# Gated delta-rule block on one core: convolution taps read an SBUF copy of the projection instead of PSUM

## The chip, the cores and the metric

The kernel runs on one core of a Trainium2 chip. A core has five engines which work side by side, each on its own in-order queue: TensorE (PE in the profile; its weight loads are PEld) multiplies matrices and writes to PSUM, VectorE (DVE), ScalarE (ACT) and GpSimd (POOL) work elementwise, and SyncE (SP) issues most of the transfers. The metric is the device time of the whole program in microseconds; less is better. Everything is 32-bit floating point.

## The reference

The input is 16 sequences of 128 tokens with 256 features. Three parts follow each other: an attention, a gated delta rule (where the change lies) and a feed-forward part with low-rank adapters and weights rounded to 8 bits. Cut to what matters here:

```python
x = x + delta_rule(attention(x, ...), W_qkv, W_z, W_b, W_a, conv_w, ...)
x = x + quantized_ffn(lora_ffn(x, ...), ...)

def delta_rule(hidden_states, ...):
    mixed = hidden_states @ W_qkv
    mixed = silu(causal_conv(mixed, conv_w))       # four taps over time, each channel by itself
    q, k, v = split(mixed)                         # 16 key heads, 32 value heads, 128 wide
    core = chunk_gated_delta_rule(q, k, v, g, beta)
    core = core * rsqrt(mean(core * core)) * norm_w * silu(z)
    return core.reshape(b, s, VAL_DIM) @ W_out

def causal_conv(x, w):
    out = xp[:, 0:s, :] * w[:, 0]                  # xp: x with three zeros in front of the time axis
    for j in range(1, 4):
        out = out + xp[:, j:j + s, :] * w[:, j]

def chunk_gated_delta_rule(q, k, v, g, beta):
    q, k = l2norm(q), l2norm(k)                    # x * rsqrt(sum(x * x) + eps)
    A = tril(-(k_beta @ k.T) * decay, -1)
    T = solve_triangular(eye - A, eye)             # the inverse of each 64-token chunk's matrix
    ...
```

## The kernel before

The delta rule is cut into 64 units, one for each of 16 key heads and each of 4 groups of 4 sequences; a unit has 8 pairs of a sequence and a value head (two value heads share a key head). A unit's work is a chain of steps over some ten slots. The loop at lines 853 to 910 makes the slots: in slot n the keys of unit n are made (`keys`, lines 471 to 510), the decays of unit n-1 are applied (`decays`, lines 512 to 545), unit n-7 gets its inverse merged and its values (`mergers`, `values`), unit n-8 its outputs, unit n-10 its last projection (`finish_unit`). In every fourth slot, and the one after, the 32x32 inverses of four units are worked out by VectorE and GpSimd (`inverse`, lines 547 to 642). For the first slots the rest of the attention is mixed in, and after the last slot comes the feed-forward part from line 915 on.

`plan` (lines 859 to 860) gives each step of a slot a due time between 0 and 24; the steps are called in the order of these times. A due time is thus a rank and not a clock. The program's framework then lists the instructions of each engine: it takes the steps' order as priority, but an instruction whose inputs it expects to be ready earlier may come ahead of one of higher priority. On the chip each engine works through its list in order and waits where an input or a buffer is missing.

The steps that the prediction speaks of:

- `conv` (lines 459 to 469) makes a projection of 128 channels by 512 tokens on TensorE into one PSUM buffer (`mm_in`, line 455), multiplies it by the last tap on ScalarE (line 464, the tile `cv`), and adds the other three taps on VectorE (line 466), each of which reads the PSUM buffer again, shifted by 1 to 3 tokens. It runs four times a slot: qk(0) and qk(1) in `keys`, val(0) and val(1) in `values` (line 715).
- `silu` (line 483) writes keys and queries to `kq`; `square` (line 487) squares all of `kq` with one instruction into a tile `sqa` of its own; `norms` (lines 489 to 495) sums the squares over the channels with products against a matrix of ones, four blocks of 32 partitions, and VectorE turns the result.
- `products` (lines 526 to 535) multiplies keys with keys and queries, and VectorE multiplies the result by the decays into `bT` and `aT`. `diagonal` sends the 32x32 diagonal blocks by four DMAs to the tile `diag`, from which `inverse` begins.
- `fades` (lines 436 to 450) prepares the decays of two units at once in every even slot: GpSimd lines 443 and 444, twice, and an exponential on ScalarE (line 448).
- `norm` in `outputs` (lines 772 to 777) scales the gated output on GpSimd; `turn` and `project` in `finish_unit` transpose it and multiply it by the output weights.
- PSUM tiles with the tag `b` share six buffers; a slot asks for 23 of them in turn. A buffer is given out again when its last reader is through. `cv` has three buffers in SBUF.
- `ffn_loads` (lines 816 to 827), called in slot 66, loads the first weights of the feed-forward part into tiles that are free by then, the first adapter among them (into `sqa`'s place) and the first group's residual (into `diag`'s place). The residuals of the other groups are loaded from line 926 on.

Of the kernel before, what the change touches and what calls it, by code (L numbers as in the profile page):

```python
# [8 lines left out]
F32 = mybir.dt.float32  # L9
I32 = mybir.dt.int32  # L10
AF = mybir.ActivationFunctionType
# [45 lines left out]
def tile_adaln_attn_ffn(  # L57
# [401 lines left out]
    def conv(g, w, blk, col):  # L459

        ps = mm_in(g, w, blk)
        cv = pc.tile([P, GS, S], F32, name="cv", tag="cv", bufs=3)
        psv = ps.rearrange("p (s t) -> p s t", t=S)
        A.activation(cv, psv, AF.Copy, scale=cw[:, col, 3:4])  # L464
        for sh in (1, 2, 3):
            V.scalar_tensor_tensor(out=cv[:, :, sh:], in0=psv[:, :, : S - sh],  # L466
                                   scalar=cw[:, col, 3 - sh : 4 - sh], in1=cv[:, :, sh:],
                                   op0=ALU.mult, op1=ALU.add)
        return cv

    def keys(u):
# [4 lines left out]
        def qk(j):  # L476

            if j == 0:
                d["kq"] = pa.tile([P, GS, 2, S], F32, name="kq", tag="kq", bufs=2)
            d["kc", j] = conv(g, w_qk[u], 1 - j, NK + kh if j == 0 else kh)  # L480

# [3 lines left out]
        def square():  # L485
            d["sqa"] = pa.tile([P, GS, 2, S], F32, name="sqa", tag="sqa")
            A.activation(d["sqa"], d["kq"], AF.Square)

        def norms():

            ps = ps_b.tile([P, 2 * GS, BL], F32, name="ps_n", tag="b")
            for b in BLOCKS:
                T.matmul(ps[b], lhsT=ones, rhs=d["sqa"][:, :, :, b], start=True, stop=True)
            d["tr"] = pc.tile([P, 2 * GS, BL], F32, name="turned", tag="turned")
            V.transpose(out=d["tr"].rearrange("p s t -> p (s t)"), in_=ps.rearrange("p s t -> p (s t)"))  # L495

        def factors():
            tr = d["tr"][:, :, 0].rearrange("p (s j) -> p j s", j=2)
            nn = d["nn"] = pc.tile([P, 2, GS], F32, name="nn", tag="nn", bufs=10)
# [207 lines left out]
    def values(u):  # L707
# [4 lines left out]
        def val(h):  # L712
            if h == 0:
                d["v"] = late["p"].tile([P, GS, 2, S], F32, name="v", tag="v", bufs=2)
            d["vT", h] = conv(g, w_v[u], h, 2 * NK + 2 * kh + h)

# [99 lines left out]
    def ffn_loads():  # L816
        def loaded(name, src, tag, **kw):
# [7 lines left out]
        adapter(0, pa.tile([P, GS * LA + LB], F32, name="adapters", tag="prod"),  # L825
                pa.tile([P, GS * LA], F32, name="firsts", tag="sqa"))()
        residual(0, pa.tile([P, GS, D], F32, name="x1_in", tag="diag"))

# [10 lines left out]
    def residual(g, t):  # L839
        nc.sync.dma_start(out=t, in_=x1[g * GS : (g + 1) * GS].rearrange("b s d -> s b d"))  # L840
        pre["x", g] = t
# [11 lines left out]
    for n in range(N + LAST):  # L853
# [31 lines left out]
        if at(MERGE) or at(MERGE + 1):  # L885
            steps = mergers(at(MERGE), at(MERGE + 1))
            plan(steps, [0, 0, 8, 14] if at(MERGE) else [14])
        if at(1):
            plan(decays(at(1)), [0, 4.5, 9, 10])
        if at(0):  # L890
            plan(keys(at(0)), [2, 5, 6.0, 10, 12.0, 14, 19])
        if n % 2 == 0 and n < N:
            plan(fades(n), [8, 12, 19])
        if at(MERGE):
            plan(values(at(MERGE)), [5.5, 8.5, 9, 15.5, 18, 23])
        if at(OUT):
            plan(outputs(at(OUT)), [13, 20, 16, 17, 19, 22, 23.5])
        if at(LAST):
            plan(finish_unit(at(LAST)), [0, 8, 14, 14])
        if at(NU + 1) and (n - NU - 1) % NU == 0:  # L900
# [14 lines left out]
    with ExitStack() as st:  # L915
# [9 lines left out]

        for g in range(1, NG):
            residual(g, w3.tile([P, GS, D], F32, name=f"x1_in{g}", tag=f"x1_in{g}"))
# [220 lines left out]
```

## Time and profile before

| | us |
|---|---|
| median of three runs | 2430.25 |
| lowest and highest run | 2428.03, 2436.76 |
| profiled execution: device time | 2431.28 |
| its span, first to last instruction | 2429.6 |
| busy: TensorE, VectorE, ScalarE, GpSimd | 2200.7, 1548.1, 1361.7, 1145.9 |
| conv: taps on VectorE, line 466 (768 instructions) | 540.2 |
| conv: scales on ScalarE, line 464 (256) | 174.5 |
| squares on ScalarE, line 487 (64) | 67.2 |

Busy time of one engine is a sum over the whole program. An instruction row names line, engine and operation, then the tile written, an arrow and the tiles read, then the sizes as partitions x elements. What stands in brackets behind a row of a timeline is the idle time of the engine before it and what ended it; a row of waits has the waiting instruction, what it waited for, and total us, times and longest wait. Matmul ends in the profile are modelled, so times between starts say more than single durations.

### The profile page before, as it was taken

What the parts mean: (1) busy time and instruction counts of PE and PEld (TensorE: products, weight loads), DVE (VectorE), ACT (ScalarE), POOL (GpSimd) and SP (SyncE); (2) the same over time, 40 slices, a digit from 0 to 9 for tenths busy, and PEclk for the clock granted to TensorE, in tenths of its full rate; (3) what the DMA queues carried; (4) which work ended last, traced back from release to release, by engine and by line L of the source; (5) the groups of instructions that cost most, each with busy time, mean ns of one, the idle gap of its engine ahead of it and who ended that gap; (6) DMA issues with size and microseconds to landing.
All of it is one profiled execution on the core that took longest, in us unless ns stands there. A gap on an engine that the chain in (4) does not pass through costs nothing. (4 is left out here: it accounts for less than half of the span.)

```text
span 2429.6 us, 41939 instructions
## 1 busy us (share of the span) xinstructions
PE 2200.7 (91%) x16248; PEld 1450.2 (60%) x16248; DVE 1548.1 (64%) x2102; ACT 1361.7 (56%) x3008; POOL 1145.9 (47%) x833
## 2 busy tenths in 40 slices
PE   7868759989999998989999998989999898999999
PEld 3433336766667666766666666766677686344445
DVE  4657878687776968687777868687876831311111
ACT  3566536766666666766666666766666574111110
POOL 4585535465555656465555656465556413700000
PEclk9889879999999999999999999999999999999999
DMA  1200022222222322322223222222322323000000
GB/s 56 91 17 15 24 56 76 70 66 71 68 66 77 104 72 64 75 68 68 68 80 86 82 73 64 77 66 68 85 69 80 89 52 123 26 0 20 9 0 18
DMA packets 289910, 148.37 MB, mean 61 GB/s; under 512 B 184241, under 2 KB 278193, under 8 KB 289713
## 3 DMA queue, kind: packets, MB, share of 16 engines
q1 hardware_dynamic: 287792, 141.44, 21.1%
q0 software_dynamic: 1344, 4.20, 0.5%
q8 instruction: 131, 2.15, 0.4%
q14 instruction: 67, 0.54, 0.1%
q10 hardware_dynamic: 576, 0.05, 0.0%
HBM read 119.13 MB, written 5.51 MB: 51 GB/s over the span
## 5 line engine op out<-in xcount | busy, mean ns | idle before, releaser
L466 DVE SCALAR_TENSOR_TENSOR cv<-ps_in,cw,cv 128x500 f32<-128x500 f32 (+2 forms) x768 | 540.2, 735 | 88.8 <-ACT cv L464 84.2
L455 PE MATMUL ps_in<-hT,w_v 128*128 128x512 f32 x512 | 281.5, 679 | 6.8 <-DVE z L770 4.6
L464 ACT ACTIVATE cv<-ps_in,cw 128x512 f32<-128x512 f32 x256 | 174.5, 682 | 182.7 <-PE ps_in L455 182.0
L770 DVE TENSOR_TENSOR z<-ps_ot,z 128x512 f32<-128x512 f32 x128 | 87.9, 687 | 289.9 <-ACT sq L768 289.9
L455 PE MATMUL ps_in<-hT,w_qk 128*128 128x512 f32 x512 | 251.3, 613 | 7.1 <-DVE z L770 6.2
L743 PE MATMUL ps_z<-w_gate,hT 128*128 128x256 f32 x1024 | 242.3, 379 | 1.7 <-DVE z L770 1.7
L800 PE MATMUL ps_out<-wo_head,zT 128*128 128x256 f32 x1024 | 238.8, 386 | 1.0 <-ACT zT L792 1.0
L500 POOL TENSOR_SCALAR nn<-turned 128x4 f32<-128x4 f32 x64 | 15.6, 244 | 419.4 <-DVE turned L495 316.8
L800 PEld LDWEIGHTS ps_out<-wo_head,zT 128*128 128x128 f32 x1024 | 189.0, 190 | 38.0 <-issue 10.7
L743 PEld LDWEIGHTS ps_z<-w_gate,hT 128*128 128x128 f32 x1024 | 189.4, 190 | 27.7 <-DVE z L770 2.6
L455 PEld LDWEIGHTS ps_in<-hT,w_v 128*128 128x128 f32 x512 | 104.6, 217 | 113.3 <-issue 105.2
L768 ACT ACTIVATE sq<-ps_ot 128x128 f32<-128x128 f32 x512 | 143.2, 280 | 31.6 <-PE ps_ot L762 23.0
L483 ACT ACTIVATE kq<-cv 128x512 f32<-128x512 f32 x128 | 80.1, 626 | 126.8 <-DVE cv L466 126.7
L756 ACT COPY y<-ps_y 128x512 f32<-128x512 f32 x128 | 75.0, 586 | 135.3 <-PE ps_y L755 130.6
L530 PEld LDWEIGHTS ps_kq<-kq 128*128 128x128 f32 x512 | 102.5, 203 | 73.4 <-issue 53.4
L455 PEld LDWEIGHTS ps_in<-hT,w_qk 128*128 128x128 f32 x512 | 94.2, 195 | 84.8 <-issue 67.0
L1055 POOL TENSOR_TENSOR o<-o,x_in 128x512 f32<-128x512 f32 x8 | 10.1, 1265 | 283.4 <-DVE o L1054 283.4
L777 POOL TENSOR_TENSOR z<-z,r 128x1024 f32<-128x1024 f32 x64 | 132.2, 2066 | 23.2 <-DVE z L770 20.4
L790 PE MATMUL ps_zt<-ident,z 128*128 128x128 f32 x512 | 88.9, 301 | 59.4 <-DVE aT L534 57.4
L530 PE MATMUL ps_kq<-kq 128*128 128x256 f32 x512 | 136.8, 391 | 0.0
L762 PE MATMUL ps_ot<-y,aT 128*128 128x128 f32 x1024 | 135.3, 275 | 0.0
L755 PEld LDWEIGHTS ps_y<-v,W 128*128 128x128 f32 x1024 | 123.3, 194 | 16.6 <-ACT W L701 10.8
(212 smaller groups left out, 5004.2 us busy)
## 6 DMA issues: line engine op xcount, KB each, us to landing
aT<-sums SPq DMA_DIRECT2D x64, 512.0 KB, 5.8
w_qk<-in_w_qkv_dram SPq DMA_DIRECT2D x128, 128.0 KB, 2.2
w_v<-in_w_qkv_dram SPq DMA_DIRECT2D x64, 256.0 KB, 2.7
w_gate<-in_w_z_dram SPq DMA_DIRECT2D x64, 256.0 KB, 2.7
wo_head<-in_w_out_dram SPq DMA_DIRECT2D x64, 256.0 KB, 2.7
diag<-bT SPq DMA_DIRECT2D x256, 32.0 KB, 2.0
W<-Uc SPq DMA_DIRECT2D x256, 32.0 KB, 2.0
T<-Tc SPq DMA_DIRECT2D x128, 32.0 KB, 1.9
```

The lines of the kernel that those rows point to most:

```text
L455: T.matmul(ps, lhsT=w[:, c, blk, :], rhs=hTs[g][:, c, :], start=c == 0, stop=c == ND - 1)
L464: A.activation(cv, psv, AF.Copy, scale=cw[:, col, 3:4])
L466: V.scalar_tensor_tensor(out=cv[:, :, sh:], in0=psv[:, :, : S - sh], scalar=cw[:, col, 3 - sh : 4 - sh], in1=cv[:, :, sh:], op0=ALU.mult, ...
L530: T.matmul(ps[:, j, :, :], lhsT=d["kq"][:, s, 0, :], rhs=d["kq"][:, s, :, :], start=True, stop=True)
L743: T.matmul(ps[:, j, :], lhsT=hTs[g][:, c, t0 : t0 + S], rhs=w_gate[u][:, c, :], start=c == 0, stop=c == ND - 1)
L755: T.matmul(ps[:, j, :], lhsT=d["W"][:, p, :], rhs=v[:, p, :], start=True, stop=True)
L762: T.matmul(ps[:, j, :], lhsT=d["aT"][:, p, :], rhs=d["y"][:, p, :], start=True, stop=True)
L768: A.activation(sq, ps[:, j, :], AF.Square, accum_out=d["r"][:, p : p + 1])
L770: V.tensor_tensor(z, ps, z, ALU.mult)
L777: G.tensor_tensor(d["z"], d["z"], d["r"][:, :, None].to_broadcast([P, NP, S]), ALU.mult)
L790: T.transpose(ps[:, j, :], d["z"][:, 4 * n + j, :], ident)
L800: T.matmul(ps[:, j, :], lhsT=d["zT", n][:, 2 * j + h, :], rhs=w_o[u][:, h, :], start=kh == j == h == 0, stop=kh == NK - 1 and j == h == 1)
```

## The change

`conv` first copies the PSUM buffer to an SBUF tile `raw` on ScalarE (four buffers). All four taps read `raw`: ScalarE's scale, and VectorE's three, whose two tensor inputs, `raw` and `cv`, are now both in SBUF. `cv` has two buffers instead of three. `conv` returns `raw` too; for keys and queries the squares are written into it, by one instruction for each, so that `sqa` goes. `norms` takes the two tiles apart, with eight products of half the width in place of four, and `factors` reads the sums in that order. The first adapter's raw rows take `diag`'s place in `ffn_loads`, and the first group's residual is loaded with the others after the slots. Most due times are changed.

```diff
     def conv(g, w, blk, col):
         ps = mm_in(g, w, blk)
-        cv = pc.tile([P, GS, S], F32, name="cv", tag="cv", bufs=3)
-        psv = ps.rearrange("p (s t) -> p s t", t=S)
-        A.activation(cv, psv, AF.Copy, scale=cw[:, col, 3:4])
+        raw = pc.tile([P, GS, S], F32, name="raw", tag="raw", bufs=4)
+        A.copy(raw, ps.rearrange("p (s t) -> p s t", t=S))
+        cv = pc.tile([P, GS, S], F32, name="cv", tag="cv", bufs=2)
+        A.activation(cv, raw, AF.Copy, scale=cw[:, col, 3:4])
         for sh in (1, 2, 3):
-            V.scalar_tensor_tensor(out=cv[:, :, sh:], in0=psv[:, :, : S - sh],
+            V.scalar_tensor_tensor(out=cv[:, :, sh:], in0=raw[:, :, : S - sh],
                                    scalar=cw[:, col, 3 - sh : 4 - sh], in1=cv[:, :, sh:],
                                    op0=ALU.mult, op1=ALU.add)
-        return cv
+        return cv, raw
...
-            d["kc", j] = conv(g, w_qk[u], 1 - j, NK + kh if j == 0 else kh)
+            d["kc", j], d["sqa", j] = conv(g, w_qk[u], 1 - j, NK + kh if j == 0 else kh)
...
         def square():
-            d["sqa"] = pa.tile([P, GS, 2, S], F32, name="sqa", tag="sqa")
-            A.activation(d["sqa"], d["kq"], AF.Square)
+            for j in range(2):
+                A.activation(d["sqa", j], d["kq"][:, :, j, :], AF.Square)
         def norms():
             ps = ps_b.tile([P, 2 * GS, BL], F32, name="ps_n", tag="b")
-            for b in BLOCKS:
-                T.matmul(ps[b], lhsT=ones, rhs=d["sqa"][:, :, :, b], start=True, stop=True)
+            for j in range(2):
+                for b in BLOCKS:
+                    T.matmul(ps[b, GS * j : GS * (j + 1), :], lhsT=ones, rhs=d["sqa", j][:, :, b], start=True, stop=True)
...
-            tr = d["tr"][:, :, 0].rearrange("p (s j) -> p j s", j=2)
+            tr = d["tr"][:, :, 0].rearrange("p (j s) -> p j s", j=2)
...
-            d["vT", h] = conv(g, w_v[u], h, 2 * NK + 2 * kh + h)
+            d["vT", h], _ = conv(g, w_v[u], h, 2 * NK + 2 * kh + h)
...
-                pa.tile([P, GS * LA], F32, name="firsts", tag="sqa"))()
-        residual(0, pa.tile([P, GS, D], F32, name="x1_in", tag="diag"))
+                pa.tile([P, GS * LA], F32, name="firsts", tag="diag"))()
...
-            plan(steps, [0, 0, 8, 14] if at(MERGE) else [14])
+            plan(steps, [1, 5, 8, 15] if at(MERGE) else [15])
         if at(1):
-            plan(decays(at(1)), [0, 4.5, 9, 10])
+            plan(decays(at(1)), [0, 2.5, 8, 13])
         if at(0):
-            plan(keys(at(0)), [2, 5, 6.0, 10, 12.0, 14, 19])
+            plan(keys(at(0)), [2, 4.5, 5.5, 10, 12.0, 14, 19])
         if n % 2 == 0 and n < N:
-            plan(fades(n), [8, 12, 19])
+            plan(fades(n), [10, 13.0, 21])
         if at(MERGE):
             plan(values(at(MERGE)), [5.5, 8.5, 9, 15.5, 18, 23])
         if at(OUT):
-            plan(outputs(at(OUT)), [13, 20, 16, 17, 19, 22, 23.5])
+            plan(outputs(at(OUT)), [15, 22, 17.5, 20, 21, 23, 24])
         if at(LAST):
-            plan(finish_unit(at(LAST)), [0, 8, 14, 14])
+            plan(finish_unit(at(LAST)), [0, 6, 11, 12])
...
-        for g in range(1, NG):
+        for g in range(NG):
             residual(g, w3.tile([P, GS, D], F32, name=f"x1_in{g}", tag=f"x1_in{g}"))
```

The lists of due times name the steps in the order in which their functions return them: `mergers` place, lower, grow, last; `decays` weight, products(0), products(1), diagonal; `keys` qk(0), qk(1), silu(0), silu(1), square, norms, factors; `fades` log(0), log(1), exp; `values` val(0), val(1), silu(0), silu(1), val_turn(0), val_turn(1); `outputs` gate(0), gate(1), new_values(0), new_values(1), attend(0), attend(1), norm; `finish_unit` turn(0), turn(1), project(0), project(1).

## The prediction

> **What bounds the kernel now.** The page comes first, for the shares; then the busy time by stretch, the waits of the tensor engine, and the timelines of four neighbouring slots.
>
> ```profile
> span 2429.6 us, 41939 instructions
> PE 2200.7 (91%) x16248; PEld 1450.2 (60%) x16248; DVE 1548.1 (64%) x2102; ACT 1361.7 (56%) x3008; POOL 1145.9 (47%) x833
> ```
>
> TensorE is nearly full, but 91% is a mean. A slot is the time from one unit's first `w_qk` product to the next one's. From about 490 us to 1858 us the slots repeat in groups of four, 12.6 groups in all; one group, busy time by stretch:
>
> ```profile
> core 0: us, PE busy (x) PEld busy (x) DVE busy (x) ACT busy (x) POOL busy (x), PEclk, DMA share, GB/s
> 984.50:1008.70 24.20, 24.20 (x226) 18.05 (x225) 12.63 (x20) 16.14 (x42) 7.93 (x8) 1.00 0.24 61
> 1008.70:1034.80 26.10, 24.69 (x227) 17.95 (x225) 21.19 (x37) 21.39 (x49) 15.84 (x13) 1.00 0.35 92
> 1034.80:1063.60 28.80, 25.98 (x224) 18.91 (x224) 28.63 (x31) 16.02 (x41) 16.41 (x10) 0.94 0.20 50
> 1063.60:1093.60 30.00, 26.76 (x225) 18.93 (x226) 19.46 (x24) 20.36 (x44) 19.67 (x15) 0.94 0.30 82
> ```
>
> Call the rows A, B, C, D. In A TensorE never pauses: 24.2 us is the price of a slot by TensorE alone. Four of them are 96.8 us; the group takes 109.1. So 12.3 us a group, 155 us in all, is the most that this stage can give. C has VectorE busy for 28.63 of 28.80 us: the inverse of the 32x32 blocks runs there. The waits of TensorE name the same place:
>
> ```profile
> PE ps_zt L790 <- DVE aT L534: 57.4, 26, 2.6
> ...
> PE ps_n L493 <- ACT sqa L487: 24.3, 22, 5.6
> PE ps_up L681 <- DVE z L770: 20.1, 13, 2.5
> ```
>
> These are PSUM buffers (six under tag `b`) which VectorE returns late. In C, VectorE's timeline and then TensorE's:
>
> ```profile
> 1040.52 1.06 DVE L578 TENSOR_TENSOR prod<-inv,gm 128x512 f32<-128x512 f32 x1
> 1041.51 0.73 DVE L466 SCALAR_TENSOR_TENSOR cv<-ps_in,cw,cv 128x508 f32<-128x508 f32 x1
> ...
> 1043.42 0.67 DVE L534 TENSOR_TENSOR aT<-ps_kq,aT 128x512 f32<-128x512 f32 x1
> ```
> ```profile
> 1044.24 1.09 PE L790 MATMUL ps_zt<-ident,z 128*128 128x128 f32 x4 [2.56 <-DVE aT L534]
> ```
>
> ScalarE had the first tap ready at 1037.47; VectorE took it up at 1041.51, 4.0 us late, and TensorE stood 2.56 us. Its next products are slow as well (the `ps_in` row after it takes 2.96 us for a usual 1.88, the clock of the stretch is 0.94): some 1.5 us more. D loses 0.3, 1.28 and 1.90 us the same way and 1.9 to the clock, B 0.71 (squares late) and 0.70.
>
> **What the Trainium skill says.** "SBUF — State Buffer", Who interferes with whom: a VectorE instruction with two SBUF inputs contends with a GpSimd instruction that reads SBUF, and the one that starts second waits until the other is through; with one SBUF input it does not. The trace agrees. The 128x128 scalar_tensor_tensor of line 330 reads two SBUF tiles:
>
> ```profile
> L330 DVE SCALAR_TENSOR_TENSOR a<-a,ea x4: 273/916/2014, 98.3 to 328.7; 128x128 f32<-128x128 f32 x4
> ```
> ```profile
> 183.05 1.90 POOL L256 TENSOR_TENSOR sc<-sc,mx 128x1024 f32<-128x1024 f32 x1 [3.90 <-PE ps_qk L202]
> ```
>
> Its slowest instance starts at 183.08 and takes 2.01 us instead of 0.27, ending just after GpSimd's. Today's taps read PSUM and one SBUF tile, and their means by form are 729 to 740 ns with no such tail. "TensorE: Matmul & The Clock Gate", What's actually happening: an idle window drops TensorE to half its clock; the slow products after the 2.56 us stall agree.
>
> **The change part by part.** The profiled execution is 2431.28 us, 1.7 outside its span; the sum starts there. The median of the runs is 2430.25.
>
> *Copies, scales, squares (ScalarE).* 256 copies of 128x512 from PSUM at 586 ns (the row of line 756) are +150 us. The 256 scales now read SBUF: today 682; the SBUF row of line 718 has 626 without a per-partition scale; I take no change, -14 to +14 us. 128 squares at about 630 (strided, as line 483) for 64 at 1050: +13. ScalarE goes from 1361.7 to some 1525 us, 63%: not a bound, but 2.6 us a slot in an in-order queue.
>
> *The taps (VectorE).* 768 instructions stay. Shorter from SBUF? Line 290 (PSUM, per-partition scalar) takes 344 at 128 elements, line 330 (SBUF, immediate) 273. At most -70 ns, 54 us of VectorE work; at worst 0. No row parts the memory from the scalar, so I take 0.
>
> *PSUM comes back earlier: gain.* Four of a slot's 23 buffers are returned by a 0.59 us copy. In C, TensorE then waits for `aT` at grow instead of turn(1): from the end of products(0) the run ahead is 1.72 + 0.63 + 1.72 + 0.49 = 4.6 us (rows of `ps_in`, `ps_lo`, `ps_in`, `ps_zt`) against 4.2 today; and bT, aT no longer stand behind two taps (1.3 us). Some 1.6 us more lateness is borne in C and in D[...]: -1.6 - 1.5 in C, -1.6 - 1.9 in D, 6.6 us a group, **if VectorE is no later than today**.
>
> *The shared port: cost.* It is later. GpSimd's timeline in B:
>
> ```profile
> 1011.40 1.90 POOL L777 TENSOR_TENSOR z<-z,r 128x1024 f32<-128x1024 f32 x1
> 1013.26 1.91 POOL L443 TENSOR_TENSOR aT<-aT,off 128x1024 f32<-128x1024 f32 x1
> 1015.24 1.10 POOL L444 TENSOR_SCALAR_AFFINE_SELECT aT<-aT 128x1024 f32<-128x1024 f32 x1
> 1016.31 1.91 POOL L443 TENSOR_TENSOR aT<-aT,off 128x1024 f32<-128x1024 f32 x1
> 1018.29 1.09 POOL L444 TENSOR_SCALAR_AFFINE_SELECT aT<-aT 128x1024 f32<-128x1024 f32 x1
> ```
>
> VectorE's taps run from 1011.45 to 1024.2. Laid side by side, the taps of the four slots overlap 15.5 us of GpSimd: some 6 each in B and D (all five instructions), 1.8 each in A and C (line 777 alone). The new due times of fades (10, 13) hardly move these: line 443 ran as soon as its DMA had landed. Each overlap becomes waiting, and GpSimd and VectorE take turns. Where it lands:
> - B. VectorE waits of itself 1.31 and 0.84 us before the inverse begins; 6 less 2.1 starts the inverse 4 us late. GpSimd, four taps (2.9 us) later, also delays ScalarE's exp, which sits in front of the last conv, the silu and the squares for norms. Its due time is now 21, which may let the squares pass. TensorE waits for norms 2.0 us longer (0 to 3.6).
> - C. 4.0 + 4 - 2.0 = 6 us late; borne 1.4 today, 3.0 now: 3.0 stall plus 1.5 clock, for 4.1 today: +0.4.
> - D. 3.1 us later against TensorE (2.0 from C, 1.5 of C's own lock, less 0.4), less the 1.6 now borne: +1.5. The earlier project (11, 12) gives norms cover: -0.6 over the group. A: 0, VectorE is idle half of it.
>
> Net +3.3 us a group (-6.6 without the lock's part, +7 with VectorE never catching up); 12.6 groups: **+42**.
>
> *cv from three buffers to two.* val's scale waits for the silu of a key's cv; val's two are held to val_turn(1), just ahead of the next qk(0). 0 in A; it is behind the lag counted in B and D.
>
> *Moved steps.* No instruction is added by the due times. TensorE's order becomes products(0), qk(1), lower, val(0), turn(1), grow, with project(0), project(1) ahead of norms and gate(0), last behind; new_values(1), attend, gate(1) later by 1 to 3 of 24. lower's ScalarE copies now follow the scale of qk(1), with grow queued behind them: 0.7 us of ScalarE work, against the 1.72 us of val(0) on TensorE: 0; if silu(0) stands in front of them and waits for a late VectorE, it is part of C's and D's lag. place at 1 puts six DMAs of SP behind one more step; what reads them (last, due 15) is half a slot away: 0. The later attend brings GpSimd's line 777 closer to the next taps; it begins with them today already.
>
> *norms.* 16 products of 128 columns for 8 of 256. The columns are the same; today's 8 take 0.57 us. Between 0 and +0.57; the 32 small `ps_lo` products need only 20 ns each, so +0.1: 64 x 0.1 = **+6**.
>
> *Before 490 us.* Six taps a slot at first, beside lines 256 and 267; VectorE is 77 to 82% busy in 200 to 400 us. Lock against earlier PSUM: **+3** (-10 to +20).
>
> *DMAs and the end.* place moves to 1, diagonal's four DMAs to 13 on SP; begin needs them a slot later. firsts takes diag's buffer, last read a slot before. residual(0) leaves SP's queue there and leads the later loads: issued about 2043.6, landing in 4.2 us by the answer for line 840, with 1.0 us of transposes done by 2049. ScalarE's copy of them started only at 2052.94 (9.41 us idle for a DMA), which hides it: 0; without that cover +3.
>
> Sum: 2431.3 + 42 + 6 + 3 = 2482, rounded down to **2478** for the taps' possible gain from SBUF.
>
> **The rivals.** *Faster (0.35):* the lock falls into idle time (VectorE is busy 82 of 109 us a group), and the inverse starts under 1.6 us late: from there on PSUM decides. Then -6.6 x 12.6 = -83, +6, a port rest of +10: 2365 (2345 to 2415). For it: A's idle VectorE; against it: GpSimd's run starts with the taps, slot after slot. *VectorE becomes the bound (0.13):* 82 + 15.5 us of work against 96.8, and its forced waits (3.72 us for `prod` in D among them): a group of 116, 2431 + 7 x 12.6 + 9 = 2528. *The copy isn't at once (0.07):* ScalarE's queue stands behind exp or a silu, buffers return as late as today, the lock hits slack: 2430.
>
> **How the numbers follow.** My case (0.45): 2478, own range 2443 to 2512. Half a per cent (12 us) is about what a measurement tells from no change. Faster 0.35, same 0.07, slower 0.45 + 0.13 = 0.58. The range leaves out a tenth at the fast rival's lower end and under a tenth of the VectorE-bound one: 2350 to 2525.
>
> **What would show it.** Taps of line 466's successor with a tail to 2.6 us and a mean near 1.0 us, GpSimd's 443, 444, 777 stretched; stretch A still near 24.3, B longest changed; TensorE's waits for `ps_zt` gone, for `ps_n` and `ps_up` larger. Wrong: taps near 735 ns throughout, or C and D near 26 us.

## The result and the profile after

The changed kernel takes 2591.39 us (median of 4 runs, 2586.66 to 2593.45) against 2430.73 on the same chip: a ratio of 1.0664, 95% interval 1.0650 to 1.0679, or +161 us. The forecast of 2478 had the direction, and less than a third of the size. From the page of the changed kernel, its span and the busy time of the engines:

```profile
span 2590.3 us, 42973 instructions
...
PE 2269.1 (88%) x16760; PEld 1496.8 (58%) x16760; DVE 1748.3 (67%) x2102; ACT 1520.8 (59%) x3326; POOL 1202.5 (46%) x833
```

ScalarE is where the sum had it (1525 forecast). VectorE is busy for 200 us more with the same 2102 instructions, and no engine is full: the instructions take longer, and the kernel waits more. The costliest groups of instructions show whose work grew (busy us and mean ns follow the bar):

```profile
L467 DVE SCALAR_TENSOR_TENSOR cv<-raw,cw,cv 128x508 f32<-128x508 f32 (+2 forms) x768 | 734.5, 971 | 58.6 <-ACT cv L465 51.2
...
L443 POOL TENSOR_TENSOR aT<-aT,off 128x1024 f32<-128x1024 f32 x64 | 140.7, 2200 | 4.3 <-DMA aT<-sums 4.3
L779 POOL TENSOR_TENSOR z<-z,r 128x1024 f32<-128x1024 f32 x64 | 139.9, 2186 | 58.2 <-DVE z L772 55.4
L444 POOL TENSOR_SCALAR_AFFINE_SELECT aT<-aT 128x1024 f32<-128x1024 f32 x64 | 91.5, 1432 | 3.4
```

The taps went from 735 to 971 ns in the mean (+181 us), GpSimd's three operations that stand beside them (in the order of these rows) from 1929, 2066 and 1124 ns to 2200, 2186 and 1432. One steady group of four slots, busy time by stretch (us, then PE, PEld, DVE, ACT, POOL with counts, granted clock, DMA share, GB/s), rows A, B, C, D as before:

```profile
1055.20:1079.50 24.30, 24.30 (x235) 18.17 (x234) 14.25 (x20) 18.93 (x48) 8.08 (x8) 1.00 0.23 59
1079.50:1110.40 30.90, 26.52 (x235) 19.80 (x234) 26.29 (x36) 23.11 (x51) 18.29 (x13) 0.94 0.28 79
1110.40:1140.00 29.60, 26.18 (x234) 18.90 (x233) 29.44 (x30) 19.04 (x47) 13.82 (x10) 0.94 0.18 45
1140.00:1174.80 34.80, 28.69 (x235) 19.98 (x234) 24.87 (x26) 22.79 (x51) 23.75 (x15) 0.85 0.29 76
```

A is as it was. B is 4.8 us longer than the row of before, D 4.8, C 0.8. The means over slots 16 to 55 say the same: A 24.34, B 30.87, C 29.82, D 34.73, together 119.8 for 109.2. By part of the program (slot starts read off the first `w_qk` product of each unit): up to slot 12 463.0 to 479.9 us (+17), slots 12 to 63 1394.8 to 1532.2 (+137), slot 63 to the last `ps_out` 188.9 to 197.8 (+9), the feed-forward part 382.9 to 380.4 (-2). The longer stalls also cost clock: over the whole span TensorE was granted 0.929 of its clock, 0.954 before. That is an estimate of 184 us of clock lost (0.071 of 2590) for 112 (0.046 of 2430), so up to 72 of the 161 us go through the clock. The waits of TensorE, and one of ScalarE:

```profile
ACT kq L484 <- DVE cv L467: 223.0, 74, 7.7
...
PE ps_kq L532 <- DVE aT L536: 60.6, 26, 3.4
...
PE ps_y L757 <- ACT W L703: 49.9, 23, 3.3
...
PE ps_zt L792 <- DVE z L772: 38.7, 10, 3.9
...
PE ps_in L455 <- DVE z L772: 25.8, 17, 4.2
...
PE ps_n L495 <- ACT raw L488: 20.5, 27, 2.3
```

Before, ScalarE's `silu` of the keys waited 126.7 us for the taps; now 223.0. TensorE's waits for VectorE moved from `ps_zt` behind `aT` to `ps_kq` behind `aT` and `ps_zt` behind `z`, and a wait for ScalarE has grown from 1.6 to 49.9 us: `ps_y` for the copy of `W`. VectorE's timeline in B, in C and in D:

```profile
1084.19 9.36 DVE L467 SCALAR_TENSOR_TENSOR cv<-raw,cw,cv 128x504 f32<-128x504 f32 x5
...
1117.68 2.40 DVE L467 SCALAR_TENSOR_TENSOR cv<-raw,cw,cv 128x508 f32<-128x508 f32 x1
...
1121.26 0.68 DVE L536 TENSOR_TENSOR aT<-ps_kq,aT 128x512 f32<-128x512 f32 x1
...
1146.92 2.29 DVE L630 TENSOR_REDUCE inv<-prod 128x128 f32<-128x2048 f32 x1 [3.60 <-POOL prod L580]
1149.24 1.94 DVE L635 STREAM_TRANSPOSE Tc<-inv 128x1024 f32<-128x1024 f32 x1
1151.07 0.64 DVE L772 TENSOR_TENSOR z<-ps_ot,z 128x512 f32<-128x512 f32 x1
```

GpSimd's timeline beside the first of these rows:

```profile
1083.38 2.04 POOL L779 TENSOR_TENSOR z<-z,r 128x1024 f32<-128x1024 f32 x1
1085.39 2.34 POOL L443 TENSOR_TENSOR aT<-aT,off 128x1024 f32<-128x1024 f32 x1
1087.80 1.42 POOL L444 TENSOR_SCALAR_AFFINE_SELECT aT<-aT 128x1024 f32<-128x1024 f32 x1
1089.20 2.33 POOL L443 TENSOR_TENSOR aT<-aT,off 128x1024 f32<-128x1024 f32 x1
1091.60 1.42 POOL L444 TENSOR_SCALAR_AFFINE_SELECT aT<-aT 128x1024 f32<-128x1024 f32 x1
```

And TensorE's timeline, the waiting rows of the same three slots:

```profile
1102.02 1.94 PE L757 MATMUL ps_y<-v,W 128*128 128x128 f32 x8 [3.29 <-ACT W L703]
...
1121.99 1.44 PE L532 MATMUL ps_kq<-kq 128*128 128x256 f32 x4 [3.42 <-DVE aT L536]
...
1151.77 1.12 PE L792 MATMUL ps_zt<-ident,z 128*128 128x128 f32 x4 [3.88 <-DVE z L772]
```

In B five taps take 9.36 us for 3.7: VectorE and GpSimd take turns, and each of the five taps ends 0.53 or 0.54 us after one of GpSimd's operations has ended. ScalarE's two `silu` instructions wait 2.17 and 2.08 us for them in its queue, everything behind is late by so much, and TensorE stands 3.29 us for the copy of `W` at the end. In C the tap at 1117.68 takes 2.40 us and TensorE stands 3.42. In D VectorE waits for GpSimd's product for the inverses, reduces it, transposes the result (line 635), and only then multiplies by `z`, which returns the PSUM buffer that TensorE has waited 3.88 us for.

### The profile page after: what moved, and what is told of

It is laid out like the page before. It is cut to its first block, busy times and chain, and to the rows that moved or that the text cites. A ratio compares the mean times of both kernels' runs of the same rounds, so it can differ in the third digit from the quotient of the medians.

```text
span 2590.3 us, 42973 instructions
## 1 busy us (share of the span) xinstructions
PE 2269.1 (88%) x16760; PEld 1496.8 (58%) x16760; DVE 1748.3 (67%) x2102; ACT 1520.8 (59%) x3326; POOL 1202.5 (46%) x833
## 5 line engine op out<-in xcount | busy, mean ns | idle before, releaser
L467 DVE SCALAR_TENSOR_TENSOR cv<-raw,cw,cv 128x508 f32<-128x508 f32 (+2 forms) x768 | 734.5, 971 | 58.6 <-ACT cv L465 51.2
L502 POOL TENSOR_SCALAR nn<-turned 128x4 f32<-128x4 f32 x64 | 27.2, 426 | 495.3 <-DVE turned L497 494.9
L745 PE MATMUL ps_z<-w_gate,hT 128*128 128x256 f32 x1024 | 251.6, 386 | 3.6 <-DVE W L687 2.5
L463 ACT COPY raw<-ps_in 128x512 f32<-128x512 f32 x256 | 148.8, 581 | 150.6 <-PE ps_in L455 144.8
L802 PEld LDWEIGHTS ps_out<-wo_head,zT 128*128 128x128 f32 x1024 | 198.3, 194 | 61.1 <-issue 35.5
L532 PE MATMUL ps_kq<-kq 128*128 128x256 f32 x512 | 159.1, 438 | 60.6 <-DVE aT L536 60.6
L484 ACT ACTIVATE kq<-cv 128x512 f32<-128x512 f32 x128 | 80.3, 628 | 223.4 <-DVE cv L467 223.0
L757 PE MATMUL ps_y<-v,W 128*128 128x128 f32 x1024 | 164.0, 307 | 50.1 <-ACT W L703 49.9
L465 ACT ACTIVATE cv<-raw,cw 128x512 f32<-128x512 f32 x256 | 184.3, 720 | 4.8
L757 PEld LDWEIGHTS ps_y<-v,W 128*128 128x128 f32 x1024 | 148.0, 217 | 67.1 <-ACT W L703 61.8
L779 POOL TENSOR_TENSOR z<-z,r 128x1024 f32<-128x1024 f32 x64 | 139.9, 2186 | 58.2 <-DVE z L772 55.4
L443 POOL TENSOR_TENSOR aT<-aT,off 128x1024 f32<-128x1024 f32 x64 | 140.7, 2200 | 4.3 <-DMA aT<-sums 4.3
```

The lines of the kernel that those rows point to most:

```text
L443: G.tensor_tensor(t4, t4, o[:, :, :, None].to_broadcast([P, NP, 2, C]), ALU.subtract)
L463: A.copy(raw, ps.rearrange("p (s t) -> p s t", t=S))
L465: A.activation(cv, raw, AF.Copy, scale=cw[:, col, 3:4])
L467: V.scalar_tensor_tensor(out=cv[:, :, sh:], in0=raw[:, :, : S - sh], scalar=cw[:, col, 3 - sh : 4 - sh], in1=cv[:, :, sh:], op0=ALU.mult, ...
L532: T.matmul(ps[:, j, :, :], lhsT=d["kq"][:, s, 0, :], rhs=d["kq"][:, s, :, :], start=True, stop=True)
L745: T.matmul(ps[:, j, :], lhsT=hTs[g][:, c, t0 : t0 + S], rhs=w_gate[u][:, c, :], start=c == 0, stop=c == ND - 1)
```

## The experiments

Two theories were there at the start. **Exclusion:** taps with two SBUF operands and GpSimd's reads shut each other out, and the delay runs down ScalarE's queue. **Order:** the new times of the steps, the copies and two buffers of `cv` make other lists and other waits, whatever the taps read. A third (ScalarE has become too slow) goes with the second. All ratios are against the kernel before on the same chip, with 95% intervals. "Copies" are ScalarE's, of the projections.

**1. The changed kernel, taps from PSUM again.**

```diff
-        A.copy(raw, ps.rearrange("p (s t) -> p s t", t=S))
+        psv = ps.rearrange("p (s t) -> p s t", t=S)
+        A.copy(raw, psv)
...
-            V.scalar_tensor_tensor(out=cv[:, :, sh:], in0=raw[:, :, : S - sh],
+            V.scalar_tensor_tensor(out=cv[:, :, sh:], in0=psv[:, :, : S - sh],
```

> The changed kernel with one thing undone: VectorE's three taps read the projection in PSUM again. The copy to SBUF by ScalarE stays, as do the scale and the squares that use it, the split norms, two buffers of cv and the new times of the steps. Theory (the taps with two SBUF operands and GpSimd's tensor operations exclude each other, and the delay passes down ScalarE's queue): the taps fall from a mean of 971 ns to 735 and GpSimd's decay subtraction from 2200 to about 1930 ns, and nearly all of the +160 us goes: 2420 to 2470 us. Rival (the new times of the steps, or the order that they give): the time stays at 2570 to 2600. Rival (ScalarE's 150 us of copies and cv with two buffers): at most the first 50 us go, 2540 to 2590.

Measured: 2511.7 us, ratio 1.0338 (1.0320 to 1.0357); taps 736 ns, line 443 at 1902. Half of the loss goes, half stays: B falls to 26.0, D stays at 35.3. Neither theory explains the loss alone.

**2. The changed kernel with the old times.** The edit puts the old lists of due times back.

> The changed kernel with the old times of the steps; all else as changed. Theory (exclusion of VectorE and GpSimd): the taps stay at 950 ns or more in the mean, and the time stays at 2550 to 2630 us. Rival (the times are the cause): 2430 to 2470. The part between (the new times put GpSimd's decays against the taps, the old ones less): 2500 to 2550, with fewer stretched taps.

Measured: 2640.8 us, 1.0865 (1.0847 to 1.0883). In this structure the new times are worth 50 us; as the only cause they are out.

**3. Both kernels with fills in place of GpSimd's work.** In each, three fills stand for lines 443 and 444 and two for the scaling of `z`, so that GpSimd is busy for about as long as with the work that is left out.

```diff
-            G.tensor_tensor(t4, t4, o[:, :, :, None].to_broadcast([P, NP, 2, C]), ALU.subtract)
-            G.affine_select(out=t[:, i], in_=t[:, i], pattern=[[0, NP], [1, S]], compare_op=ALU.is_ge,
-                            fill=-1e30, base=0, channel_multiplier=-1)
+            for _ in range(3):
+                G.memset(t[:, i], -1.0)
...
-            G.tensor_tensor(d["z"], d["z"], d["r"][:, :, None].to_broadcast([P, NP, S]), ALU.mult)
+            for _ in range(2):
+                G.memset(d["z"], 0.01)
```

> The changed kernel with GpSimd's operations on the decays and on z replaced by fills of about the same number, which read nothing (the preparation of the decays and the scaling of z are left out of the computation). Theory: without GpSimd reading SBUF the taps fall to 740 ns in the mean though they read SBUF, and the time is within 1% of the kernel before with the same fills, about 2400 to 2440 us. Rivals (times of the steps, ScalarE's added copies, two buffers of cv): the distance of some 6% between changed and unchanged kernel stays, so 2540 us or more here against 2400 there.

> The kernel before with the same fills in place of GpSimd's operations on the decays and on z (that preparation and scaling are left out). It is the base for the changed kernel with fills. All theories: taps at 735 ns, 2390 to 2435 us, since GpSimd's work was hidden before; what it gains is to be taken off the other one.

Measured: 2495.8 us (1.0271, 1.0253 to 1.0289) changed, 2422.9 (0.9967, 0.9953 to 0.9981) before. The changed kernel gains 96 us, the other 8; 73 us lie between them still. The expectation of under 1% missed: there is a second cause.

**4. The new times, the copies, or the rest of the change.** Three runs: the kernel before with the new times alone; with copies alone (below, old times, taps on PSUM); the changed kernel without copies.

```diff
-        A.activation(cv, psv, AF.Copy, scale=cw[:, col, 3:4])
+        raw = pc.tile([P, GS, S], F32, name="raw", tag="raw")
+        A.copy(raw, psv)
+        A.activation(cv, raw, AF.Copy, scale=cw[:, col, 3:4])
```

> The kernel before with nothing changed but the times of the steps, which are the new ones. The taps from PSUM in the changed kernel left 81 of its 160 us. If the new order of the steps is the cause of those (in the fourth slot TensorE waits 3.9 us for the product with z), this shows them by itself: 2490 to 2520 us, with that slot at 34 us or more. If ScalarE's copies are the cause: 2425 to 2445, with that slot near 30.

> The kernel before with one thing added: ScalarE copies each projection to SBUF and its scale reads the copy; VectorE's taps stay on PSUM, and the old times, three buffers of cv and the squares' own tile stay. If ScalarE's 150 us of copies are the cause of the other half: 2480 to 2530 us. If the order of the steps is: 2432 to 2450, the copies being hidden but for a scale that comes 0.6 us later.

> The changed kernel without the copies: scale and taps read PSUM; the new times, two buffers of cv and the split squares and norms stay. With the copies and taps from PSUM it took 2512 us. If the copies are the cause of what is left: 2430 to 2450. If the order of the steps or two buffers of cv are: 2490 to 2512.

Measured: 2589.8 (1.0657, 1.0640 to 1.0675), 2565.7 (1.0551, 1.0533 to 1.0569), 2505.2 (1.0303, 1.0284 to 1.0321). The two single edits cost 159 and 135 us, both beyond what was expected, and together with the rest and with taps on PSUM they cost 81: they don't add up. The waits of TensorE with the new times alone:

```profile
PE ps_n L493 <- ACT sqa L487: 113.5, 44, 10.2
...
PE ps_in L455 <- DVE z L770: 85.0, 27, 3.5
```

and with the copies alone:

```profile
PE ps_lv L699 <- ACT T L685: 40.0, 14, 3.9
```

Each single edit has a wait of its own, which is small where the parts stand together: `ps_n` waits 17.2 us in the run without copies, and `ps_lv` waits for no copy of `T` in experiment 1. Every one of these edits changes the lists of TensorE, VectorE and ScalarE in hundreds or thousands of places, because the framework lists instructions by when it expects their inputs. So none of these runs, experiment 1 included, holds the order fixed.

**5. Half of the taps.** The changed kernel, the values' taps on PSUM, the keys' on the copy.

> The changed kernel with half of the taps undone: those of the values read PSUM, those of the keys and queries still read the copy. The exclusion of VectorE and GpSimd is worth 80 us by the run with all taps on PSUM. If it is a matter of how many instructions are met: half of it, 2540 to 2560 us. If it is one place (the keys' taps stand beside GpSimd's z and decays in the second slot of the group): 2570 to 2592 if the keys' taps make it, 2510 to 2530 if the values' do.

Measured: 2560.1 us, 1.0528 (1.0510 to 1.0546). Groups of instructions:

```profile
L469 DVE SCALAR_TENSOR_TENSOR cv<-raw,cw,cv 128x508 f32<-128x508 f32 (+2 forms) x384 | 446.8, 1176 | 7.1 <-ACT cv L467 3.5
...
L469 DVE SCALAR_TENSOR_TENSOR cv<-ps_in,cw,cv 128x508 f32<-128x508 f32 (+2 forms) x384 | 280.0, 733 | 60.1 <-ACT cv L467 54.0
```

Keys' taps stretched by 441 ns each make 169 of the 181 us of lost VectorE time, and B stays at 30.83: they meet GpSimd's run. Of the 31 us gained, C gives 2.8 us a group (29.8 to 27.1), D takes 1.2 back, and 6 us come before slot 12. So the loss doesn't follow the count of stretched taps: the values' taps carry 12 of the 181 us, and taking them off gains 31. How much of this is their place and how much the new lists, this run doesn't tell.

**6. The exclusion at a fixed order.** A fill for each of lines 443, 444 and 779 (777 in the kernel before), one for one, leaves the lists of all engines in both kernels as they were, place by place, but for the operation that GpSimd does there.

```diff
-            G.tensor_tensor(t4, t4, o[:, :, :, None].to_broadcast([P, NP, 2, C]), ALU.subtract)
-            G.affine_select(out=t[:, i], in_=t[:, i], pattern=[[0, NP], [1, S]], compare_op=ALU.is_ge,
-                            fill=-1e30, base=0, channel_multiplier=-1)
+            G.memset(t[:, i], -1.0)
+            G.memset(t[:, i],
+                     -1.0)
...
-            G.tensor_tensor(d["z"], d["z"], d["r"][:, :, None].to_broadcast([P, NP, S]), ALU.mult)
+            G.memset(d["z"], 0.01)
```

> The changed kernel with GpSimd's three operations on the decays and on z replaced one for one by fills that read nothing (that preparation and scaling are left out). Every engine's list of instructions keeps its order, which the earlier runs did not: nothing differs but what GpSimd reads and how long it works. Theory (half of the +160 us is the exclusion between GpSimd's reads and taps with two SBUF operands, the other half is the new order of the lists): the taps fall to 735 to 760 ns, the second slot of the group to 26 to 27 us, and the time to 2490 to 2515 us. If the exclusion makes all of the loss: 2425 to 2450. If the exclusion's delay is hidden and the order makes all: 2575 or more.

> The kernel before with the same fills one for one, in the same order (the same parts are left out): the base for the changed kernel with them. GpSimd's work is hidden in it, but for some 1 us in places where GpSimd's own product for the inverses comes earlier: 2405 to 2432 us by all theories.

Measured: 2471.0 us (1.0178, 1.0158 to 1.0198) changed, 2406.8 (0.9917, 0.9894 to 0.9940) before. The fills also take less time (0.95 us for 1.1 to 2.1), which is worth 24 us before and is taken off: 120 - 24 = **96 us of the 161 are the exclusion between the taps and these three operations**, with all that follows from it. The shorter work could be worth more than 24 us in the changed kernel. Against that stands experiment 3, where the fills are about as long as the work: 96 - 8 = 88 us, though with other lists. By part: 4 of the 17 us up to slot 12, 88 of 137 in the slots to 63, 5 or 6 of 9 after. The taps of the changed kernel with fills:

```profile
L467 DVE SCALAR_TENSOR_TENSOR cv<-raw,cw,cv 128x508 f32<-128x508 f32 (+2 forms) x768 | 573.2, 758 | 54.0 <-ACT cv L465 43.2
```

the five taps of B in VectorE's timeline, in the same place of the list as those of 9.36 us:

```profile
1132.84 3.87 DVE L467 SCALAR_TENSOR_TENSOR cv<-raw,cw,cv 128x504 f32<-128x504 f32 x5
```

These fills write and don't read; that taps and fills pass each other agrees with the Trainium skill, "SBUF — State Buffer", Who interferes with whom, by which a GpSimd instruction that only writes does not contend with VectorE's second input. From slot 12 on the taps take 737 ns in the mean; the rest of the 758 lies before. TensorE's waits in the changed kernel with fills, and then in the kernel before with fills:

```profile
PE ps_in L455 <- DVE z L772: 41.9, 20, 3.9
...
PE ps_kq L532 <- DVE aT L536: 30.2, 24, 1.8
PE ps_vt L726 <- ACT cv L720: 29.7, 17, 2.2
...
PE ps_zt L792 <- DVE z L772: 26.0, 11, 3.9
```
```profile
PE ps_zt L790 <- DVE aT L534: 57.5, 26, 2.6
...
PE ps_up L681 <- DVE z L770: 20.1, 13, 2.4
...
PE ps_in L455 <- DVE z L770: 15.1, 16, 2.9
```

The waits for `aT` fall from 57.5 to 30.2 us, as they should when buffers come back earlier. The waits for the product with `z` rise from 35.2 to 67.9, most of it in D, and 29.7 us for the values' `silu` are new, 2.1 us in each B: there the last tap of the values stands behind the first steps of the inverses on VectorE.

Means of the slots: A 24.32, B 28.20, C 26.91, D 33.28, against 24.22, 25.38, 28.86, 30.41 in the kernel before with fills. So the exclusion is +2.2 us in B, +2.9 in C, +1.6 in D (6.7 a group). Without it, C would be 2.0 us shorter than before, but B 2.8 and D 2.9 longer: 3.8 us a group, 48 us, which the exclusion of the taps doesn't make. They are left for the order, the buffers and the copies.

**7. What holds D.** In both kernels the product with `z` stands behind VectorE's last reduction for the inverses, and that waits for GpSimd. VectorE's timeline in a D of the kernel before:

```profile
1177.16 2.29 DVE L628 TENSOR_REDUCE inv<-prod 128x128 f32<-128x2048 f32 x1 [3.72 <-POOL prod L578]
1179.36 0.68 DVE L770 TENSOR_TENSOR z<-ps_ot,z 128x512 f32<-128x512 f32 x1
```

In the changed kernel, with fills or without, two things have come between in eight of the ten groups from slot 16 to 55. One is the transpose of line 635 (1.9 us), which stands between the reduction and the product with `z`. The other is an exclusion in a new place: VectorE's product of 1024 elements for the same merge now starts just behind a multiplication of GpSimd (line 524) and takes 3.5 us for 1.9. Before, then after:

```profile
1061.07 1.92 DVE L578 TENSOR_TENSOR Tc<-inv,gm 128x1024 f32<-128x1024 f32 x1
```
```profile
1137.97 3.50 DVE L580 TENSOR_TENSOR Tc<-inv,gm 128x1024 f32<-128x1024 f32 x1
```
```profile
1137.79 1.90 POOL L524 TENSOR_TENSOR aT<-aT,c 128x1024 f32<-128x1024 f32 x1
```

The product with `z` so ends 10.5 to 13.4 us into D with fills, where it ended 7.7 to 8.8 us into it in the kernel before with fills. No run takes one of the two away by itself.

A fill of the same tile in place of GpSimd's product leaves out the last merge's larger half, and keeps the order on every engine; one run on top of experiment 1, one on the kernel before.

```diff
-                times(t, *args, G if part else V)
+                G.memset(t, 0.0) if second and part else times(t, *args, G if part else V)
```

> The changed kernel with the taps on PSUM (2512 us) and one thing more: GpSimd's product of 2048 elements for the last merge of the inverses is a fill of the same tile (the inverses are not the reference's), all lists in the same order. VectorE's reduction of it waits 3.7 us for GpSimd, and the product with z, which frees a PSUM buffer that TensorE waits for in the fourth slot of the group, stands behind this reduction. If this is what makes that slot 35 us long: it falls to 30 to 31.5 us and the time to 2440 to 2470. If something else holds the slot: 2495 or more.

> The kernel before with the same fill in place of GpSimd's product (the inverses are not the reference's), all lists in the same order. Here TensorE waited only 1.3 us in the fourth slot for the product with z. If the same wait is behind it, the slot falls from 30.2 to 28 to 29.5 us and the time to 2405 to 2425; the gain is then much smaller than in the changed kernel, and the difference of the two gains is what the new order costs there.

Measured: 2460.6 us (1.0130, 1.0105 to 1.0155), 51 less than experiment 1, with D at 33.0 for 35.3; and 2365.3 (0.9735, 0.9719 to 0.9752), 65 less than before, with D at 26.5 for 30.2. The wait holds D in both, and the unchanged kernel gains more from its removal, not less as expected: the wait by itself doesn't make the difference between the two kernels. What else keeps D at 33 in the kernel of experiment 1 shows in its waits: `ps_n`, for the squares, rises from 39.6 to 55.3 us.

**8. Copies by times, and the buffers of `cv`.** With taps on PSUM, two buffers of `cv` and split squares and norms in all four:

| | old times | new times |
|---|---|---|
| no copies | 2501.1 | 2505.2 |
| copies | 2574.4 | 2511.7 |

> The kernel before with two buffers of cv, split squares in four buffers of their own and split norms; no copies, taps on PSUM, old times. It parts these from the new times: with the new times the same structure took 2505 us. If the new times make the rest of the loss: 2430 to 2445 us here. If two buffers of cv or the split norms do: 2490 or more. If each edit costs because the lists are made anew: between, and with no pattern among the four combinations of times and copies.

> The changed kernel with taps on PSUM and the old times. With the new times it took 2512 us, the kernel before with copies alone and old times 2566. If the copies with the old times make ScalarE late (TensorE waits for its copies of T): 2540 to 2580 us, and the new times gain 30 to 70. If two buffers of cv and the split norms were what helped: 2500 to 2520.

Their ratios are 1.0296 (1.0273 to 1.0319) and 1.0592 (1.0572 to 1.0611). With the old times the copies cost 73 us, with the new ones 7: that is what the new times do. But 71 us are there without copies and with the old times. Of what is left in that run, the buffers were taken alone:

```diff
-        cv = pc.tile([P, GS, S], F32, name="cv", tag="cv", bufs=3)
+        cv = pc.tile([P, GS, S], F32, name="cv", tag="cv", bufs=2)
```

> The kernel before with two buffers of cv in place of three, nothing else. Two buffers, split squares and split norms together cost 71 us with the old times. The prediction put the buffers at nothing: 2428 to 2436 us. If they are what costs: 2480 to 2505; then the split squares and norms are nearly free.

Measured: 2514.3 us, 1.0334 (1.0309 to 1.0358): +84. Split squares and norms, put on top of it, gave 13 back. ScalarE's timeline in a slot B of the kernel before (it starts at 1117.8) and of this one (1163.6); the row of line 464 is the third projection's scale, line 448 the exponential of the decays:

```profile
1124.40 0.67 ACT L464 ACTIVATE cv<-ps_in,cw 128x512 f32<-128x512 f32 x1
...
1128.49 1.91 ACT L448 ACTIVATE aT<-aT 128x2048 f32<-128x2048 f32 x1 [0.77 <-POOL aT L444]
```
```profile
1174.24 1.91 ACT L448 ACTIVATE aT<-aT 128x2048 f32<-128x2048 f32 x1 [2.68 <-POOL aT L444]
1176.06 0.67 ACT L464 ACTIVATE cv<-ps_in,cw 128x512 f32<-128x512 f32 x1
```

With three buffers the scale runs 6.6 us into the slot; with two it is listed behind the exponential, which waits for GpSimd, and runs 12.5 us into it, with the merger's copies and a projection's taps behind it. Three buffers of `cv` beside four of `raw` don't fit into SBUF. Three beside three take the same room as the change; no run has them, so the price of this buffer within the changed kernel isn't shown.

**9. Which of the new times.** Experiment 1 with the old times of the output steps.

```diff
-            plan(outputs(at(OUT)), [15, 22, 17.5, 20, 21, 23, 24])
+            plan(outputs(at(OUT)), [13, 20, 16, 17, 19, 22, 23.5])
```

> The changed kernel with taps on PSUM (2512 us) and the old times of the output steps alone. The new ones make the products with y and z later, so that the product with z on VectorE, which gives a PSUM buffer back, comes later in the next slot. If that is why the fourth slot of the group is 35 us long with the new times and 30 to 33 with the old: it falls to 31 to 33 and the time to 2455 to 2485 us. If another of the new times does it (the merger's steps, now behind the first projection): 2500 to 2520.

Measured: 2555.5 us, 1.0526 (1.0500 to 1.0551). The idea falls: D stays at 34.5 us and A, B and C together lose 4.2. The old output times are worse beside the rest of the new ones.

**10. A version that beats both.** The last merge of the inverses, dealt out the other way: VectorE makes the product of 2048 elements first, GpSimd that of 1024. The same arithmetic.

```diff
-            st_["t"] = ts = []
-            for part in range(2):
+            st_["t"] = ts = {}
+            for part in ((1, 0) if second else (0, 1)):
...
-                times(t, *args, G if part else V)
-                ts.append(t)
+                times(t, *args, G if part != second else V)
+                ts[part] = t
...
-                 lambda: products16(True), lambda: sums16(True, 0), lambda: sums16(True, 1), end_t, end_u])
+                 lambda: products16(True), lambda: sums16(True, 1), lambda: sums16(True, 0), end_t, end_u])
```

> The kernel before with the last merge of the inverses dealt out the other way: VectorE makes the product of 2048 elements first, GpSimd the one of 1024, and the sums follow in this order; the same arithmetic. GpSimd's product of 2048 took 7.3 us and VectorE's reduction waited 3.7 us for it; with a fill in its place the kernel took 2365 us. VectorE's chain to the last reduction gets 1.4 us shorter (3.8 + 2.7 + 1.2 us for 1.9 + 1.2 + 3.7 + 2.3), and both products with z stand before it in VectorE's list: 2370 to 2405 us. If the lists made anew cost more than this gains: 2430 or more.

> The changed kernel with the same exchange. If its fourth slot is held by the product with z behind the reduction: 2530 to 2565 us; the exclusion in the second slot of the group stays, so it remains over 5% above the kernel before with the exchange. If its other waits take the place: 2580 or more.

Measured: on the kernel before 2402.0 us, 0.9879 (0.9859 to 0.9899), the fastest with the whole computation; on the changed kernel 2591.2, no gain. Two stretches of the first, C and D:

```profile
1131.80:1162.40 30.60, 24.88 (x225) 18.23 (x225) 30.43 (x31) 18.25 (x46) 18.21 (x10) 1.00 0.26 68
1162.40:1188.80 26.40, 26.32 (x225) 19.02 (x226) 19.68 (x24) 18.60 (x39) 16.77 (x15) 0.94 0.22 57
```

D falls by 3.2 us in the mean (30.25 to 27.04), C, now full of VectorE's work, rises by 1.7: 1.5 us a group, 19 of the 28 us. In the changed kernel other waits take the place, `ps_n` for the squares first (20.5 to 61.1 us).

## Why the prediction was right or wrong

- **Slower, and by the exclusion: right, but not the whole of it.** The tail of the taps (2.6 us said; up to 2.40 from slot 12 on, 5.4 and 5.7 in two taps before it), their mean (1.0 us said, 971 ns measured), the stretched lines of GpSimd, A unchanged, the wait of `ps_zt` for `aT` gone, B the most changed (+5.0 us in the mean, D +4.5): as written. `ps_n` and `ps_up` were to wait longer: `ps_n` fell from 24.3 to 20.5, `ps_up` left the list, and `ps_y` and `ps_kq` came in their place.
- **Size of the exclusion: too large rather than too small.** The sum had -6.6 us a group without it and +3.3 with it, so 9.9 for it; 6.7 at the fixed order. As the difference of the sum with it and without it, it stood at 2.0 in B, 3.5 in C and 5.0 in D, less 0.6 for the earlier `project`; measured 2.2, 2.9 and 1.6. So D is where it was too large: the taps were to be blocked there for 6 us as in B, and were for 3.0 in the mean, for 5.7 in B (1.6 in C and 1.1 in A, for 1.8 each).
- **The step that failed: the base without the exclusion.** The sum took PSUM's earlier return as -6.6 us a group, `cv` with two buffers as 0 and the moved steps as 0 (-0.6 for the earlier `project`). At the fixed order, without the exclusion of the taps, the group is 3.8 us longer than before. C did gain, 2.0 of 3.1 said; D, where 3.5 were to be gained, lost 2.9; B, where nothing was to change, lost 2.8. With 0.4 us for the norms, which the sum counted apart, that is 10 us a group off, 126 us in 12.6 groups; the exclusion's 3.2 us too many take 40 back, and up to slot 12 and after slot 63 another 14 and 9 are missing: 109 of the 113 us between 2478 and 2591. The forecast was thus nearer than its parts: two errors of opposite sign cancelled in part.
- **What the base had wrong.** It followed conv's four buffers, and they did come back earlier: TensorE's stalls for `aT` fell from 2.6 to 1.4 us in C and from 1.9 to 0.8 in D, at the fixed order. But in D the next buffer that TensorE needed was that of the product with `z`, which no copy returns and which now came later (experiment 7): stalls of 4.4 us a group for it, for 1.7. The clock came back only in part: the sum took back 1.5 us of it in C and 1.9 in D; 0.9 came back in C, 0.3 more was lost in D and 1.0 more in B. (All are means over slots 16 to 55, both kernels with fills.)
- **`cv` from three buffers to two, "behind the lag counted in B and D": wrong.** Alone it costs 84 us with the old times. What the prediction missed is that a buffer's return also sets where the framework lists the instruction that needs it: the scale went behind an exponential that waits for GpSimd.
- **Moved steps as 0: wrong as a method.** The prediction followed each step's wait on the old lists. The lists are made anew by every edit of the steps and buffers; the new times alone cost 159 us in the old structure and gain 63 in that with copies. The walk along the old timeline did not give that.
- **Before 490 us: +3 said (-10 to +20), +17 measured to slot 12.** The fills give 4 of it back, but they leave the GpSimd lines that the prediction named here (256, 267) and the inverses' products as they are, and the taps up to slot 12 still take 893 ns in the mean beside them (991 in the changed kernel). With all taps on PSUM 11.5 of the 17 us are gone, with other lists. So more than 4 us of it may be exclusion; no run parts it.
- **ScalarE +150, +13; norms +6; the taps no faster from SBUF; the end 0: right.** The copies are 148.8 us. The squares rose from 67.2 to 76.9 us, the scales from 682 to 720 ns (+10 us, inside the -14 to +14 given). A's +0.11 us fits the norms' price of 0.1, the taps' median is still 740 ns, the feed-forward part is 2 us shorter.
- **The rivals.** "Faster" needed VectorE's lateness hidden and the group at -6.6; with the exclusion of the taps taken out the kernel is still 2.7% slower than the kernel before with the same fills (2471.0 to 2406.8 us), so it was wrong by its base too. "VectorE becomes the bound" (group of 116, 2528 us) came nearest in size, but C is the only slot that VectorE fills.

How the 65 us beyond the exclusion of the taps divide between two buffers, the new times and the copies inside the changed kernel stays open. Each costs more than 65 us alone, and less together; the runs show that the parts aren't additive, and which waits are left (`z` in D, the values' `silu` in B), but not which part makes which wait.

## What to carry to other kernels

Before an operand is moved from PSUM to SBUF, lay VectorE's new two-SBUF instructions beside those of GpSimd that read SBUF, count the overlap as lost on both, and follow the in-order queues behind them. When a buffer comes back earlier, ask which buffer is waited for next, and who returns that one. A buffer taken away for the copy has a price of its own: look at what is listed behind the instruction that now waits for it. Where a framework orders the lists, an edit of one part is a new order for all; test a cause with an edit that leaves the lists as they are, like a fill for an operation of the same engine.

## What the runs showed of the hardware that was not expected

- The two engines take turns rather than one starving: five taps (3.9 us beside fills) and five operations of GpSimd (8.0 beside taps from PSUM, 1011.40 to 1019.38 before) took 10.2 us together (1083.38 to 1093.55), and both end late.
- The exclusion was there before the change, among the inverses, and the order of the starts decides who is blocked. In the kernel before, VectorE's product of 1024 elements takes 1.9 us where it starts 0.04 us ahead of GpSimd's of 2048, which then takes 7.3. Where GpSimd's has started first, it takes 5.6 and VectorE's 6.3. With a fill in GpSimd's place (experiment 7) VectorE's takes 1.9 us every time.
- The granted clock fell to half for 3.4 us not only at the stall of 2.56 us in C of the kernel before, but also 0.6 us after the end of the stall of 1.90 us in D (1074.6 to 1078.0).
- A tap costs the same from SBUF as from PSUM: the form of 504 elements takes 736 ns in the mean from the copy with fills beside it (experiment 6), and 736 ns from PSUM in the kernel before.
